# One more operand pair of a two-level Strassen-Winograd product goes by seven products instead of eight

## The chip, the cores and the metric

The kernel runs on one core of a Trainium2 chip. A core has five engines with a queue each: TensorE (PE, matrix products into PSUM), VectorE (DVE), ScalarE (ACT), GpSimd (POOL) and SyncE (SP). SP, ACT and POOL issue DMAs, which run on the core's sixteen DMA engines. PSUM has eight banks, and a 128x512 tile of float32 fills one. The metric is the device time of one launch in microseconds (us); less is better.

## The reference

A pre-norm block on x of 2 x 2048 x 512, in float32: x + attention(layernorm(x)), then x + feed-forward(layernorm(x)). The attention is over features, not positions, so it comes down to a few 512x512 products for each batch, and one product of all rows with a 512x512 matrix. The feed-forward is what the change touches:

```python
w = lut[idx]                      # 16 entries; gate, up: 1376 x 512, down: 512 x 1376
gate = einsum('bsh,oh->bso', x, w_gate)
up   = einsum('bsh,oh->bso', x, w_up)
h = silu(gate) * up
out = einsum('bsh,oh->bso', h, w_down)
```

## The kernel before

**Stages.** Layernorm and Gram matrices of x, the 512x512 products of the attention, its product with all rows (to about 287 us of the profile), gate and up (to 748 us), gate and up of the last 96 rows of the weights (to 790 us), the down product (to the end).

**Seven products for eight.** Two matrices cut in 2 x 2 blocks are multiplied by the Winograd form of Strassen's method: seven block products, named by their operand pairs 11·11, 12·21, 22·T4, S1·T1, S2·T2, S3·T3 and S4·22, and sums of blocks before and after. S are sums of blocks of the left operand (the weights), T of the right (the normed rows).

**Gate and up.** 11 tiles f of the weights' rows (the last one is short and goes another way), 4 pairs p of chunks of 1024 rows of x. The unit (f, p), class `GateUp`, makes gate and up of tile f for two chunks of 512 rows: the blocks' rows are gate and up, their columns the chunks, and the contraction (512) is cut in two. A block product is two matmuls of 128x128 weights with 128x512 rows. Stage methods `a1`, `c1`, `a2`, `c2`, `b`, `a3`, `a4` hold one block product each, with the copy out of PSUM (ScalarE) or the sum (VectorE) that follows; `silu`, `first`, `end`, `out` are the elementwise ends, which store h to DRAM from SP's queue.

**The second level.** From f = 2 on four units (f, p), (f, p+1), (f+1, p), (f+1, p+1), with f and p even, form a group, with the roles 0, 1, 2, 3. For one operand pair the products of the four units are again a 2 x 2 block product, of 128x128 and 128x512 blocks, so seven matmuls do for eight. Class `Second` does this for 12·21 (`of_b`), 22·T4 (`of_c`) and S4·22 (`of_d`). Its own right sums T1, T2, T4 are made once for each pair of p (`sums`, method `made`), put in DRAM (`far`) and loaded back for each group by ScalarE's queue (`load`). Its left sums are made for each pair of f (`sums_left`). A group runs role 0, role 1 (of both pairs of p), then roles 2 and 3. What roles 2 and 3 need of role 1's products (`r6`, `r5`) goes to DRAM: `part` copies the PSUM bank to SBUF and stores it from ScalarE's queue, role 2 adds to it with an accumulating DMA from GpSimd's queue (`onto=True`), and it comes back either with an accumulating DMA into a tile (`add_part`, of_b into `p1`, of_c into `u2`) or plain (`back`, of_d, into `y`), all from GpSimd's queue.

**Order.** The order on PE, ACT, DVE and SP is written out by hand: `Line.run` puts the stages of a unit among those of the unit before it. Between stages stands `between`, which issues one waiting load (`to_load`), one waiting set of sums (`todo`), and fills VectorE with the lookup of the weights (`fill`), as long as a planner's clock says that VectorE is less than `leads[0]` us ahead of TensorE. GpSimd's order is the framework's. DMAs of SP and ACT share eight semaphores in turn, those of POOL have eight others.

**Buffers.** PSUM: two banks "a", two "c", one each of "b", "x" (of_b), "z" (of_c), "w" (of_d). SBUF: eight buffers for T (`TT`), three for the copies of parts (`RT`), one each for `p1`, `p7`, `h1`, `y`. The class `LastRows` uses the rows again after of_b, of_c and of_d changed some blocks in place (`b12 = b22 - b12`), so it has weights of its own for the chunks concerned. The class `Down` runs through the same `Line`.

## Time and profile before

| what | value |
| --- | --- |
| median of 3 runs | 1063.71 us (1063.35 to 1063.77) |
| the profiled execution: its own time | 1064.37 us |
| its span, first to last instruction | 1062.6 us |
| instructions | 11343 |
| mean DMA rate over the span | 183 GB/s |
| a 128x512 sum on VectorE (L172), mean | 0.68 to 0.69 us |
| a 128x512 copy on ScalarE (L181, L1014), mean | 0.586 us |

The profile is of one execution. A group row has busy time, mean time of one, and the idle time of the engine before it with what ended it. An engine's idle time costs nothing unless the chain that ended last goes through it. Slices are 40 equal parts of the span; a digit is the busy share in tenths, PEclk the granted clock. A row of windows gives the length, then busy us of each engine with the number of its instructions, the granted clock, the mean busy share of the sixteen DMA engines and GB/s. A DMA issue is listed with the size and the median time from issue to landing.

### The profile page before, as it was taken

What the parts mean: (1) busy time and instruction counts of PE and PEld (TensorE: products, weight loads), DVE (VectorE), ACT (ScalarE), POOL (GpSimd) and SP (SyncE); (2) the same over time, 40 slices, a digit from 0 to 9 for tenths busy, and PEclk for the clock granted to TensorE, in tenths of its full rate; (3) what the DMA queues carried; (4) which work ended last, traced back from release to release, by engine and by line L of the source; (5) the groups of instructions that cost most, each with busy time, mean ns of one, the idle gap of its engine ahead of it and who ended that gap; (6) DMA issues with size and microseconds to landing.
All of it is one profiled execution on the core that took longest, in us unless ns stands there. A gap on an engine that the chain in (4) does not pass through costs nothing.

```text
span 1062.6 us, 11343 instructions
## 1 busy us (share of the span) xinstructions
PE 1055.5 (99%) x3554; PEld 661.3 (62%) x3554; DVE 803.3 (76%) x1538; ACT 385.1 (36%) x725; POOL 108.6 (10%) x160
## 2 busy tenths in 40 slices
PE   8999999999999999999999999999999999999998
PEld 5668887444444444444444444444998888888887
DVE  7888788898998897887988868849756455656554
ACT  4652532455542224444443444444222222211111
POOL 0000000012120120230141023014000000000000
PEclk9999999999999999999999999999999999999999
DMA  8650314589571366696697679569747665666773
GB/s 342 224 186 21 74 25 119 137 225 250 153 217 41 133 232 197 166 201 209 198 188 215 199 170 222 190 205 195 238 149 244 204 211 187 194 195 203 226 227 117
DMA packets 129084, 194.69 MB, mean 183 GB/s; under 512 B 18992, under 2 KB 59184, under 8 KB 127872
## 3 DMA queue, kind: packets, MB, share of 16 engines
q1 hardware_dynamic: 75904, 105.81, 31.4%
q0 software_dynamic: 15776, 39.92, 17.9%
q10 hardware_dynamic: 37344, 48.24, 14.0%
q8 instruction: 28, 0.46, 0.2%
q14 instruction: 32, 0.26, 0.1%
HBM read 111.42 MB, written 82.51 MB: 183 GB/s over the span
## 4 chain that ended last, share of the span: by engine, by line
PE 97%; DVE 1%; ACT 1%; DMA 0%; issue 0%; SPq 0%; ACTq 0%
PE a_g L1065 22%; PE a_d L1065 14%; PE y L839 10%; PE c_g L1065 8%; PE c_d L1065 7%; PE gp L522 6%; PE rows L1349 4%; PE b_d L1065 4%; PE x_g L1065 4%; PE z_g L1065 4%; PE w_g L1065 3%; PE b_g L1065 2%; PE ea_t L675 1%; PE ea_p L675 1%; PE ea_m L675 1%; PE ea_s L675 1%
## 5 line engine op out<-in xcount | busy, mean ns | idle before, releaser
L839 PE MATMUL y<-m,nT 128*128 128x512 f32 x256 | 110.2, 592 | 0.0
L342 DVE COPY_PREDICATED w<-b_w,w 128x1024 f32<-128x1024 int16 (+1 forms) x77 | 98.6, 1280 | 1.4
L839 PEld LDWEIGHTS y<-m,nT 128*128 128x128 f32 x256 | 48.5, 190 | 60.5 <-issue 57.3
L1065 PE MATMUL a_g<-xT_a,s 128*128 128x512 f32 x160 | 75.5, 594 | 0.0
L1065 PE MATMUL a_g<-xb,w 128*128 128x512 f32 x160 | 75.3, 593 | 0.0
L1065 PE MATMUL c_g<-xb,w 128*128 128x512 f32 x160 | 75.2, 592 | 0.0
L1065 PE MATMUL a_d<-dT,hs_a 128*128 128x256 f32 x288 | 72.6, 379 | 0.0
L522 PE MATMUL gp<-xn_a 128*128 128x128 f32 (+3 forms) x256 | 69.9, 434 | 1.7 <-DVE xn_a L223 1.7
L330 DVE TENSOR_SCALAR w<-idx_w,lut_x,lut_sb 128x1024 int32<-128x1024 int32 (+1 forms) x88 | 67.7, 794 | 0.2
L522 PEld LDWEIGHTS gp<-xn_a 128*128 128x128 f32 x256 | 43.9, 190 | 28.4 <-issue 15.1
L172 DVE TENSOR_TENSOR r<-r,p_d 128x256 f32<-128x256 f32 x64 | 27.1, 424 | 44.4 <-ACT p_d L181 41.5
L1065 PEld LDWEIGHTS a_d<-dT,hs_a 128*128 128x128 f32 x288 | 54.5, 189 | 7.7
L1065 PE MATMUL a_g<-xT_sq,s 128*128 128x512 f32 x120 | 56.7, 595 | 0.0
L181 ACT COPY p_d<-a_d 128x256 f32<-128x256 f32 x32 | 11.9, 372 | 121.4 <-PE a_d L1065 121.4
L1065 PEld LDWEIGHTS a_g<-xT_a,s 128*128 128x128 f32 x160 | 30.1, 190 | 38.9 <-issue 36.4
L1065 PEld LDWEIGHTS a_g<-xb,w 128*128 128x128 f32 x160 | 30.3, 190 | 38.5 <-issue 35.9
L1065 PEld LDWEIGHTS c_g<-xb,w 128*128 128x128 f32 x160 | 30.4, 190 | 38.3 <-issue 37.3
L342 DVE COPY_PREDICATED wd<-b_wd,wd 128x1024 f32<-128x1024 int16 (+1 forms) x42 | 50.7, 1208 | 0.8
L172 DVE TENSOR_TENSOR r<-r,a_d 128x256 f32<-128x256 f32 x64 | 26.8, 419 | 29.5 <-PE a_d L1065 29.5
L181 ACT COPY u<-a_g 128x512 f32<-128x512 f32 x40 | 23.4, 586 | 59.9 <-PE a_g L1065 57.3
L172 DVE TENSOR_TENSOR c<-a_g,p 128x512 f32<-128x512 f32 x40 | 27.6, 691 | 20.4 <-PE a_g L1065 19.0
L1349 PEld LDWEIGHTS rows<-last,xb 128*128 128x128 f32 x256 | 41.7, 190 | 0.5 <-issue 0.5
(357 smaller groups left out, 2086.2 us busy)
## 6 DMA issues: line engine op xcount, KB each, us to landing
hd<-h SPq DMA_DIRECT2D x80, 256.0 KB, 3.3
h<-hd SPq DMA_DIRECT2D x40, 512.0 KB, 6.3
nl<-nd SPq DMA_DIRECT2D x32, 256.0 KB, 5.8
xnd<-xn_f ACTq DMA_DIRECT2D x16, 512.0 KB, 4.6
fl<-xnd POOLq DMA_DIRECT2D x32, 256.0 KB, 6.1
xn_back<-xnd SPq DMA_DIRECT2D x32, 256.0 KB, 4.0
rd<-r SPq DMA_DIRECT2D x32, 256.0 KB, 3.2
r<-rd SPq DMA_DIRECT2D x32, 256.0 KB, 4.5
```

The source lines that it names most:

```text
L172: nc.vector.tensor_tensor(dest, a, b, op)
L181: nc.scalar.copy(dest, a)
L330: vec.tensor_scalar(dest.bitcast(I32), idx, lut_x[:rows, k : k + 1], lut_i[:rows, at : at + 1], ALU.bitwise_and, ALU.bitwise_xor,)
L342: vec.copy_predicated(dest, masks[level - 1], t)
L522: nc.tensor.matmul(gp[b][i][:, i * P :], xn[:, i, j % 2, :], xn[:, i:, j % 2, :], start=c % CPB == 0 and j == 0, stop=c % CPB == CPB - 1 a ...
L675: nc.tensor.matmul(ps[:, m, :], self.a[a][:, k, m * P : (m + 1) * P], self.b[b][:, k, :], start=first and m == k == 0, stop=k == 1, skip_g ...
L839: nc.tensor.matmul(ys[k], nTs[k][:, i, :], m[:, i, :], start=(i == 0), stop=(i == KB - 1))
L1065: nc.tensor.matmul(ps, lhsT, rhs, start=first and i == 0, stop=i == len(pairs) - 1, skip_group_check=not first,)
L1349: nc.tensor.matmul(ps[:, jj, :], x[:, j * P : (j + 1) * P], w, start=i == 0, stop=i == len(pairs) - 1,)
```

## The change

S3·T3 becomes a fourth `Second`, `of_e`, with the PSUM bank "e", which "c" gives up. In role 0 its first product is copied from "e" to "c" (`c0`), and `c1` adds to it there; role 1 has two kept products of it and `e4`, roles 2 and 3 get their S3·T3 as returns of `of_e` into `p7` (asked for by SP's queue before the unit begins, two buffers), role 2 with `e3` added. `of_d`'s returns go into `h1` (two buffers, SP's queue) and `y` is gone. T has five buffers instead of eight, and the loads of a group come in two lots: five in the unit before role 1, the rest within it. The copies of parts have four buffers, which the making of T uses too. `Line.run` is written anew for the roles. The planner's lead is 1.7 instead of 1.4 us. `LastRows` gets one more sum, since of_e changes T3 in place, and its sums are put on the list after the first product of the last rows.

```diff
     def psum(tag, name):
-        return fps.tile([P, E], F32, tag=tag, name=name, bufs=2 if tag in "ac" else 1)
+        return fps.tile([P, E], F32, tag=tag, name=name, bufs=2 if tag == "a" else 1)
...
-                r[tag] = x2p.tile([P, CH], F32, tag="tt", name=f"{tag}_{self.name}{g}", bufs=TT)
+                r[tag] = x2p.tile([P, CH], F32, tag="rt", name=f"{tag}_{self.name}{g}", bufs=RT)
...
-        def back(self, u):
-
-            t = u.temp("y")
-            nc.gpsimd.dma_start(t, self.parts[u.p // 2, {2: "r6", 3: "r5"}[u.role]])
+        def back(self, u, tag):
+            t = u.temp(tag, 2)
+            nc.sync.dma_start(t, self.parts[u.p // 2, {2: "r6", 3: "r5"}[u.role]])
             return t
-    RT, TT = 3, 8
+    RT, TT = 4, 5
...
-    seconds = [of_c, of_b, of_d]
+    of_e = Second("e", "e", lambda f: in_two(gu[f]["S3"]), lambda p: in_two(xs[p]["T3"]))
+    seconds = [of_c, of_b, of_e, of_d]
...
+    def loads(f, p, late=False):
         g = p // 2
+        order = []
         if 1 < f < NFT - 1 and f % 2 == 0 and p % 2:
-            order = [(of_c, "T2"), (of_c, "T1")]
-            order += [(o, tag) for tag in ("T2", "T1") for o in (of_d, of_b)]
-        elif 1 < f < NFT - 1 and f % 2 and p % 2 == 0:
-            order = [(o, "T4") for o in seconds]
+            order = [(o, tag) for tag in ("T2", "T1") for o in (of_c, of_e)]
+            order += [(of_d, "T2"), (of_b, "T2"), (of_d, "T1"), (of_b, "T1")]
+            order = order[TT:] if late else order[:TT]
+        elif 1 < f < NFT - 1 and f % 2 and p % 2 == 0 and not late:
+            order = [(o, "T4") for o in (of_e, of_b, of_c, of_d)]
...
         def c1(self):
-            self.c = self.view("c")
-            mm(self.c, self.pairs("S3", "T3"), True)
-            self.p7 = self.temp("p7")
+            if self.role is None:
+                self.c = self.view("c")
+                mm(self.c, self.pairs("S3", "T3"), True)
+            else:
+                mm(self.c, of_e.pair(self, "12", "21"), False)
+            self.p7 = self.temp("p7", 2)
             evict(self.p7, self.c)
...
+        def c0(self):
+            of_e.begin(self, "11", "11")
+            self.c = self.view("c")
+            evict(self.c, of_e.ps)
+        def kept(self, o, a, b, tag, onto=False):
+            (o.begin if onto else o.go_on)(self, a, b)
+            o.part(self, tag, onto)
+        def c4(self):
+            of_c.go_on(self, "S4", "22")
+            add(self.u2, of_c.ps, self.u2)
+        def e4(self):
+            of_e.go_on(self, "S4", "22")
+            self.p7 = self.temp("p7", 2)
+            evict(self.p7, of_e.ps)
+            add(self.u2, of_e.ps, self.u2)
+        def e3(self):
+            of_e.go_on(self, "22", "T4")
+            add(self.p7, of_e.ps, self.p7)
+        def c3(self):
+            of_c.go_on(self, "22", "T4")
+        def y_kept(self):
+            add(self.h1, of_d.ps, self.h1)
...
         def run(self, u, final=False):
...
+            after = before == 3 and role == 0
+            if not after:
+                of_last("silu")
             u.a1()
+            if role == 3:
+                u.h1 = of_d.back(u, "h1")
+                last.c3()
+                last.y_kept()
+                go(0.0)
+                u.a2()
+                go(0.0)
+                of_last("a4", "first")
+                go(0.0)
+                last.end()
+                go()
+                last.out()
+                u.a3()
+                go()
+                u.b()
+                go()
+                return
+            go()
             if before == 1:
                 last.first()
+            if role == 1:
+                u.kept(of_c, "S2", "T2", "r6")
+                go()
+                u.kept(of_e, "S2", "T2", "r6")
+            elif role == 2:
+                u.kept(of_c, "S3", "T3", "r5", True)
+                go()
+                u.kept(of_e, "S3", "T3", "r5", True)
+                u.kept(of_b, "S3", "T3", "r5", True)
+            else:
+                u.c1() if role is None else u.c0()
+                if after:
+                    last.silu()
+                go()
+            if last is not None:
+                last.a4()
+                if role == 2:
+                    u.h1 = of_d.back(u, "h1")
+                go()
+            if role == 1:
+                u.kept(of_c, "S1", "T1", "r5")
+            u.a2()
+            go()
+            if before == 3:
+                last.first()
+            if role == 1:
+                u.kept(of_e, "S1", "T1", "r5")
+                u.kept(of_d, "S2", "T2", "r6")
+                u.kept(of_b, "S2", "T2", "r6")
+                u.c4()
+            elif role == 2:
+                u.kept(of_d, "S3", "T3", "r5", True)
+                u.e3()
...
+            if role == 1:
+                u.e4()
+                u.kept(of_d, "S1", "T1", "r5")
+                u.kept(of_b, "S1", "T1", "r5")
...
-    leads = [1.4]
+    leads = [1.7]
...
-        to_load[:] = loads(*following)
+        to_load[:] = loads(f, p, late=True) + loads(*following)
...
-        u = GateUp(f, p)
+        u = next_unit or GateUp(f, p)
         line.run(u)
+        next_unit = GateUp(*following) if following[0] < NFT - 1 else None
+        if next_unit and next_unit.role in (2, 3):
+            next_unit.p7 = of_e.back(next_unit, "p7")
```

## The prediction

> **What bounds the kernel now.** I read the page first (busy shares, slices, the chain that ended last), then the chain in order of time, then the windows by stage, the DMA queues of one stretch, and the timeline of ScalarE where a unit hands over to the next.
>
> ```profile
> PE 1055.5 (99%) x3554; PEld 661.3 (62%) x3554; DVE 803.3 (76%) x1538; ACT 385.1 (36%) x725; POOL 108.6 (10%) x160
> ...
> PEclk9999999999999999999999999999999999999999
> DMA  8650314589571366696697679569747665666773
> ...
> PE 97%; DVE 1%; ACT 1%; DMA 0%; issue 0%; SPq 0%; ACTq 0%
> ```
>
> TensorE is busy 99% of the span at full granted clock, and the chain is TensorE for 97% of it. No other engine is over 76%. One piece of the chain gives the price of a product:
>
> ```profile
> 180.06 106.44 PE y L839 x248
> ```
>
> Each product has two records, so 128x512 costs 106.44 / 124 = 0.858 us. The gate-and-up units run back to back (a window row: span, then busy us of PE, PEld, DVE, ACT, POOL, then clock, DMA share, GB/s):
>
> ```profile
> 290.00:380.00 90.00, 90.00 (x211) 39.66 (x210) 81.28 (x118) 29.45 (x50) 13.34 (x24) 1.00 0.44 137
> 400.00:748.00 348.00, 348.00 (x812) 153.21 (x811) 283.54 (x424) 151.30 (x256) 71.58 (x89) 1.00 0.75 197
> ```
>
> From 400 to 748 us, where units go in groups of four, TensorE has no gap at all. A product taken out there is worth its 0.858 us, unless something that was covered comes out.
>
> **Removed: eight products.** A group has 56 products less one for each operand pair that already goes by seven (12·21, 22·T4, S4·22): 53. With S3·T3 it is 52. There are four pairs of f and two of p, so eight groups: the instruction lists have 699 products of 128x512 before and 691 after. 8 x 0.858 = 6.87 us, all on the path, and no more, since TensorE has no gap in this stage that could close besides. Group by role (0 to 3): 14, 17, 14, 8 products before, 14, 18, 14, 6 after. So roles 2 and 3 shrink from 22 to 20 products, 18.9 to 17.2 us, and role 1 grows.
>
> The Trainium skill, page Perfetto Trace Analysis, section Identifying the Most-Contended Engine, says that matmul busy time is a poor measure and weight loads are a good one. They fill 153.21 of 348 us here, so by the page TensorE has room and the sum could be 0; the row of 348.00 busy in 348.00 and the even 0.858 us speak for 6.87.
>
> **Added on VectorE and ScalarE.** VectorE gets 16 more 128x512 (0.69 us), 16 of 128x128 (0.28) and one of 128x192 (0.35): 15.9 us. Eight of the large ones and the first four of the small are a one-time set of sums near 380 to 410; the others are 2.5 us in each 91 us of a pair of f. VectorE is idle 64 of 348 us, so cover is there; without it 15.9 us is the most. ScalarE gets 16 more copies at 0.586 (9.4 us) and 40 more DMA issues at 0.33, on 151 of 348 us. The tightest place is role 1: eight kept copies, each followed by its store, in 18 products (15.4 us). Before, six followed each other as close as the matmuls came. Counting copies of 0.59 and issues of 0.45 from the rows, the last kept copy ends within 0.3 us of the product that needs its bank, when p is 3 and the cast of 1.03 us falls in there. I charge 0 and keep 0.3 x 4 = 1.2 us as its upper end. The lead of 1.7 for 1.4 lets VectorE queue 0.3 us more ahead of a result. The shortest way back is `c22` before the unit's own `a4`: in f 0 and 1 that sum ended at 298.5 and the `a4` began at 300.45, 1.9 us of cover; from f 2 on it is five products now, 4.3 us, where it was six or seven and f 0 has four. I charge 0.
>
> Bank "c" has one buffer now. In units of f 0 and 1 the sum that frees it started at 390.45 and took 0.69; the next `c1` began at 395.73. That is 4.6 us of cover; it costs nothing.
>
> **Right operands through five buffers.** Of eight T1 and T2 loads three go out within role 1. T2 of b waits on ScalarE's queue for the first z product (three products into the unit); behind it stands the copy of that very product, so nothing else is held up. It is used eight products later, 6.9 us. Landings of these loads had medians from 2.7 to 6.0 us: covered, by 0.5 us at worst.
>
> **Moved and added DMAs.** d's returns (16) go from GpSimd's queue to SP's, 16 returns of e join them there, GpSimd gets 8 accumulates more, ScalarE's queue 24 loads and 16 stores. A return waits on SP for the accumulate that feeds it; behind it stand the stores of h and the next return. In roles 2 and 3 this counts:
>
> ```profile
> 442.00:480.00 38.00, 38.00 (x89) 16.55 (x88) 33.46 (x57) 15.84 (x27) 13.55 (x17) 1.00 0.96 209
> ...
> 427.00:447.00 20.00, 20.00 (x48) 8.93 (x47) 17.62 (x22) 8.53 (x15) 5.61 (x7) 1.00 0.61 148
> ```
>
> ```profile
> q0 software_dynamic: 2272, 4.72, 72.0%
> q1 hardware_dynamic: 1080, 1.95, 14.4%
> q10 hardware_dynamic: 688, 1.27, 9.1%
> ...
> u<-part_r_c POOLq DMA_DIRECT2D x4, 256.0 KB, 5.1
> p<-part_r_b POOLq DMA_DIRECT2D x3, 256.0 KB, 4.7
> ...
> part_r_d<-r_d POOLq DMA_DIRECT2D x2, 256.0 KB, 7.2
> ```
>
> These are the DMA queues from 442 to 480 us, two times roles 2 and 3. The DMA engines are busy 0.96 of it. A plain 256 KB took (5.5 + 3.5) us / 3.22 MB, 0.73 us of all sixteen engines; GpSimd's queue had 27.4 us for 18 transfers by its bytes, 5 plain and 13 accumulating, so an accumulate is 1.8 us. The change adds here two accumulates (3.6), four returns (2.9) and a load (0.7) to 36.4 us: 43.6 us in a stretch that shrinks to 40 products, 34.3 us. Of the windows of 2 us from 436 to 492 us one had 1.21 and no other was over 1.10. At 1.05 the work lasts 41.5 us: some 7 us spill into roles 0 and 1, whose share was 0.61. They have the room; the question is who waits meanwhile.
>
> Two rules bear on this. The row is the share of 0.96, which leaves no second road. The skill's page DMA: Bandwidth & Descriptors, section Issuing engines are not separate DMA queues, says the same and speaks against the change: transfers from all queues interleave on the same sixteen engines, and moving returns to SP saves issue time only. The skill's page Perfetto Trace Analysis, sections Identifying the Most-Contended Engine and Engine Utilization, would judge DMA by HBM traffic instead, against 358 GB/s; 209 GB/s rising to an estimated 290 is below that, by which nothing is late and the gain is whole.
>
> The first to be hit is the hand-over from role 3 to role 2:
>
> ```profile
> 540.29 0.59 ACT L181 COPY p<-a_g 128x512 f32<-128x512 f32 x1 [2.08 <-PE a_g L1065]
> ...
> 547.09 0.63 ACT L1183 ACTIVATE h<-p 128x512 f32<-128x512 f32 x1 [1.15 <-DMA p<-part_r_b]
> 548.16 0.59 ACT L181 COPY p<-a_g 128x512 f32<-128x512 f32 x1 [0.43 <-PE a_g L1065]
> ```
>
> ScalarE waits at the Silu for the accumulate into p1; behind it stands the next unit's copy of p1, and TensorE's `a2` waits for that. Role 3 began at 538.38, that `a2` at 551.34: 12.9 us. Now role 3 has 8 products and `a2` comes after 5 more: 11.2 us. The copy ends 2.5 us in; the accumulate landed 4.8 us after its issue (542.27 to 547.09), so at 7.3, or 0.9 later like another one (450.02 to 455.7); Silu, copy and 0.2 of handover end at 8.7 to 9.6. Slack: 1.6 to 2.5 us, where it was 2.8. By that place about half of the spill, 3.5 us, has built up, but much of it is stores of h and loads for the next unit. So a stall is between 0 and 2 us for each of the four pairs of f. I take 0.27, near the lower end, since before no wait in these stretches reached TensorE. Role 3 before role 0 has its Silu later, behind one more product, and `a2` needs no such copy behind it: 0. The returns: e's is asked for before the unit begins and read after `e3`, ten products in (8.6 us), against landings of 4.6 to 5.1 us of d's returns before; where VectorE still waits, `c22` stands behind it, and TensorE writes its bank again eight products after `e3`. d's for role 3 waits on SP for an accumulate of role 2 and may land 1 to 2 us late; what is late then is a bank that TensorE needs 13 products on. Both 0.
>
> **Sum.** Against the profiled execution's own 1064.37 us (span 1062.6, 1.77 outside): 1064.37 - 6.87 + 4 x 0.27 = 1058.6. That execution stood 0.66 over the median of 1063.71, so 1057.9.
>
> **Rivals.** *DMA late (slower).* The accumulate into p1 lands over 2 us later than before, ScalarE sits at the Silu, TensorE at `a2`. Price if the 7 us spill reaches TensorE but for 2 us of slack: 4 x 5 = 20 us, 1077. It decides from 1.7 us for each pair (6.87 / 4). For it: 43.6 us of transfers in 34.3. Against: half of them have no reader near, and the landings of 4.7 to 7.2 us before were at a share of 0.96 already. *Gain eaten (no change).* 1.2 to 2.2 us for each pair, from that stall, ScalarE's tight role 1 and late returns together; or products that go without TensorE getting shorter. 1061.6 to 1065.8. Against: 348.00 busy in 348.00.
>
> **How the numbers follow.** Measurement tells 0.2% (2.1 us) from no change. Forecast, 0.76: 1056.3 (whole gain, less the half us by which runs differ) to 1061.5. Gain eaten, 0.10. DMA late, 0.14. The range 1056.3 to 1063.5 leaves out the last and half of the second. Faster 0.76, same 0.10, slower 0.14.
>
> **What would show it.** Right: 104 products in each pair of f, 89.3 us where it was 91.2; TensorE busy in all of the stage; DMA share near 1.0 in roles 2 and 3 and above 0.7 in 0 and 1. Wrong: TensorE waits for ScalarE's p1 copy behind a Silu that waits for a DMA; then the landing of p1's accumulate is over 7 us.

## The result and the profile after

The changed kernel took 1069.05 us (median of 4, 1067.85 to 1070.81), the kernel before 1063.65 in the same comparison (1063.35 to 1063.77). The ratio is 1.0053, interval 1.0035 to 1.0070: slower by half a per cent. Forecast were 1057.9 us, 1056.3 to 1063.5, and "faster" with 0.76.

The profiled execution took 1067.85 us (span 1066.1), the fastest of the four: it is 3.5 us over the one of the kernel before where the medians are 5.4 apart, so some 2 us of the loss are not in this trace. First the page of the changed kernel: its busy shares and its DMA slices.

```profile
PE 1052.6 (99%) x3538; PEld 655.6 (62%) x3538; DVE 815.5 (76%) x1571; ACT 390.9 (37%) x741; POOL 107.2 (10%) x158
...
DMA  8750314589671376896798699679847665666773
```

The sixteen matmul records are gone (3554 to 3538) and TensorE is still called 99% busy, so this part of the page doesn't say where the time went. The starts of TensorE's records do: in gate and up they follow each other by 0.429 us where nothing holds them. From the first record of gate and up to the first of the last rows it was 461.22 us before and is 465.23 now, 4.01 more. Sixteen records less are 6.87; so 10.88 us of gaps came in. Summed up, all that exceeds 0.429 was 1.17 us before and is 12.05 now: 39 gaps of 0.06 to 0.15 us (10 before) with 3.7 us in all, and ten longer ones with 8.2. The stages behind kept their lengths (down: 269.38 and 269.38 us between its first record and its last); gate and up began 0.5 us sooner. TensorE's waits in the changed kernel (us in total, times, longest) name the longer ones:

```profile
PE a_g L1065 <- ACT p L181: 3.7, 2, 2.8
PE a_g L1065 <- DVE h L172: 1.9, 3, 1.1
...
PE c_g L1065 <- ACT p L181: 0.7, 1, 0.7
```

Windows: one pair of f of the changed kernel, its two times roles 2 and 3, and those of the kernel before. The columns are those of the windows in the prediction.

```profile
400.00:491.00 91.00, 90.28 (x207) 38.06 (x206) 74.56 (x122) 41.28 (x71) 17.29 (x21) 1.00 0.85 250
436.00:472.00 36.00, 35.97 (x84) 15.30 (x83) 28.98 (x43) 14.64 (x26) 14.06 (x17) 1.00 1.01 257
```

```profile
436.00:472.00 36.00, 36.00 (x85) 15.69 (x83) 31.22 (x54) 16.05 (x27) 14.47 (x17) 1.00 0.90 187
```

The DMA share from 436 to 472 us is 1.01, where 0.90 was (the 0.96 of the prediction is from 442 to 480), and landings there are longer. The last column of these DMA issues, from 433 to 476 us of the changed kernel, is the median time from issue to landing:

```profile
hd<-h SPq DMA_DIRECT2D x7, 256.0 KB, 6.7
...
p<-part_r_b POOLq DMA_DIRECT2D x4, 256.0 KB, 5.5
h<-part_r_d SPq DMA_DIRECT2D x4, 256.0 KB, 6.4
u<-part_r_c POOLq DMA_DIRECT2D x4, 256.0 KB, 7.9
```

Before, from 436 to 480 us, the store of h took 3.9, p1's accumulate 4.5, d's return 5.1 and u2's accumulate 5.1. Now three kinds of place where a late landing or a short cover reaches TensorE. *A, a return of d.* The timeline of SP's queue, VectorE and TensorE at the end of the first pair of f:

```profile
464.66 0.32 SPq L1030 DMA_DIRECT2D h<-part_r_d  x1
```

```profile
470.93 0.69 DVE L172 TENSOR_TENSOR h<-w_g,h 128x512 f32<-128x512 f32 x1 [2.65 <-DMA h<-part_r_d]
471.54 0.28 DVE L172 TENSOR_TENSOR lc<-w 128x128 f32<-128x128 f32 x1
...
473.20 0.28 DVE L172 TENSOR_TENSOR lb<-w,lb 128x128 f32<-128x128 f32 x1
473.40 0.68 DVE L172 TENSOR_TENSOR h<-a_g,h 128x512 f32<-128x512 f32 x1
```

```profile
474.13 1.98 PE L1065 MATMUL a_g<-xb,w 128*128 128x512 f32 x4 [0.48 <-DVE h L172]
```

The return loads into h1, which has two buffers. It is issued at 464.66, when the store of h from two units before has landed, and lands 6.3 us later. VectorE waits for it in `y_kept`. Behind that stand eight small sums of the fillers and then the sum of `a4`, which frees bank "a" for the next f's `a1`. The same pattern costs 0.65 us here, 1.28 at 565 and 0.49 at 656.

*B, p1's accumulate.* Timelines of GpSimd, ScalarE and TensorE at the last hand-over from role 3 to role 2:

```profile
728.35 0.87 POOL L1026 DMA_DIRECT2D p<-part_r_b  x1 [7.22 <-DMA part_r_b<-r_b]
```

```profile
735.55 0.63 ACT L1178 ACTIVATE h<-p 128x512 f32<-128x512 f32 x1 [5.97 <-DMA T_d_in<-far_d1T]
736.21 0.58 ACT L181 COPY p<-a_g 128x512 f32<-128x512 f32 x1
...
736.85 1.13 PE L1065 MATMUL a_g<-xT_a,s 128*128 128x512 f32 x2 [2.79 <-ACT p L181]
```

GpSimd issues the accumulate late, because it waits for b's own accumulate in DRAM; it lands after 7.2 us, ScalarE has waited 5.97 us at the Silu, and p1's copy behind it holds TensorE. (The profile names the load that ended at the same time; the Silu reads only p1.)

*C, one product of cover.* TensorE through a role 3, first before, then after:

```profile
466.19 1.88 PE L1065 MATMUL a_g<-xb,w 128*128 128x512 f32 x4
467.91 1.88 PE L1065 MATMUL c_g<-xb,w 128*128 128x512 f32 x4
469.63 1.88 PE L1065 MATMUL a_g<-xT_x,s 128*128 128x512 f32 x4
```

```profile
466.45 1.88 PE L1065 MATMUL a_g<-xb,w 128*128 128x512 f32 x4
468.17 1.02 PE L1065 MATMUL z_g<-T_c_in,w 128*128 128x512 f32 x2
469.03 1.96 PE L1065 MATMUL a_g<-xT_x,s 128*128 128x512 f32 x4
```

Between `a1` and `a2` ScalarE copies the bank (0.58). Before, `c1` stood between with two products, 1.72 us; now it is `c3` with one, 0.86. Copy and hand-over fill that to the edge: `a2` takes 1.96 for 1.88, one of the 39 small gaps, and whatever else ScalarE has in hand goes straight to TensorE: 1.05 us at 746, where two copies of the last rows' weights stand before p1's copy. The kernel before shows the same mark: eight of its ten small gaps are at `a3` of role 3, where only one product stands between `a2` and `a3` in both kernels.

Bank "c" in role 0 is another such place. Its copy into `p7` stands between `c1` and `c2`. TensorE in the third unit of f = 8 (role 0 of its second group), before and after, then ScalarE after:

```profile
684.74 1.02 PE L1065 MATMUL c_g<-xb,w 128*128 128x512 f32 x2
...
688.17 1.02 PE L1065 MATMUL z_g<-xT_sq,w 128*128 128x512 f32 x2
689.03 1.02 PE L1065 MATMUL c_g<-xT_sq,w 128*128 128x512 f32 x2
```

```profile
688.09 1.02 PE L1065 MATMUL c_g<-xb,w 128*128 128x512 f32 x2
688.94 1.02 PE L1065 MATMUL z_g<-xT_sq,w 128*128 128x512 f32 x2
690.70 1.13 PE L1065 MATMUL c_g<-xT_sq,w 128*128 128x512 f32 x2 [0.74 <-ACT p L181]
```

```profile
689.12 1.04 ACT L303 CAST b_wd<-idx_wd 128x1024 int16<-128x1024 int32 x1 [0.25 <-DMA idx_wd<-in_down_idx_dram]
690.07 0.58 ACT L181 COPY p<-c_g 128x512 f32<-128x512 f32 x1
```

Before, `a4` and `a2` stood between as well; now only the product into "z" does. In seven of the eight roles 0 `c2` has a small gap of 0.085, and here, where a cast stands before the copy, it is 0.9 late.

### The profile page after: what moved, and what is told of

Read it like the earlier page. It is cut to its first block, busy times and chain, and to the rows that moved or that the text cites. A ratio compares the mean times of both kernels' runs of the same rounds, so it can differ in the third digit from the quotient of the medians.

```text
span 1066.1 us, 11473 instructions
## 1 busy us (share of the span) xinstructions
PE 1052.6 (99%) x3538; PEld 655.6 (62%) x3538; DVE 815.5 (76%) x1571; ACT 390.9 (37%) x741; POOL 107.2 (10%) x158
## 5 line engine op out<-in xcount | busy, mean ns | idle before, releaser
L1065 PEld LDWEIGHTS a_g<-xb,w 128*128 128x128 f32 x160 | 30.1, 190 | 41.4 <-issue 34.9
L172 DVE TENSOR_TENSOR h<-a_g,h 128x512 f32<-128x512 f32 x32 | 22.1, 689 | 35.7 <-ACT h L181 19.6
L1383 PE MATMUL rows<-last,xb 128*128 128x192 f32 x256 | 41.8, 326 | 0.0
L1065 PEld LDWEIGHTS a_g<-xT_sq,s 128*128 128x128 f32 x120 | 22.2, 190 | 29.8 <-issue 25.1
```

The lines of the kernel that those rows point to most:

```text
L172: nc.vector.tensor_tensor(dest, a, b, op)
L1065: nc.tensor.matmul(ps, lhsT, rhs, start=first and i == 0, stop=i == len(pairs) - 1, skip_group_check=not first,)
L1383: nc.tensor.matmul(ps[:, jj, :], x[:, j * P : (j + 1) * P], w, start=i == 0, stop=i == len(pairs) - 1,)
```

## The experiments

Each run was timed over some rounds beside the kernel before. "Over before" is the median less the median of before in the same comparison; the changed kernel stands at +5.4. Excess is the sum of the gaps in gate and up in the profiled execution (1.17 before, 12.05 in the changed kernel). The theory I began with: the DMA engines are overfull in roles 2 and 3, and the late landings are the stalls. The rival: the order and the covers on ScalarE and VectorE.

| run | median us | ratio, 95% interval | over before | excess |
| --- | --- | --- | --- | --- |
| e_no_traffic | 1066.72 | 1.0025 [1.0016, 1.0035] | +2.9 | 11.4 |
| e_no_accum | 1068.68 | 1.0041 [1.0030, 1.0053] | +4.9 | 14.8 |
| e_loose_return | 1069.55 | 1.0051 [1.0038, 1.0063] | +5.7 | 12.8 |
| b_first | 1070.21 | 1.0062 [1.0050, 1.0074] | +6.4 | 13.8 |
| no_sums_by_dma | 1062.82 | 0.9989 [0.9981, 0.9998] | -1.0 | 6.3 |
| y_late | 1066.88 | 1.0028 [1.0019, 1.0038] | +3.1 | 14.0 |
| h1_three | 1068.77 | 1.0043 [1.0030, 1.0056] | +4.9 | 13.3 |
| p1_two_silu | 1080.34 | 1.0149 [1.0131, 1.0168] | +16.5 | 25.9 |
| before_busy | 1065.14 | 1.0011 [1.0002, 1.0020] | +1.3 | 2.4 |
| banks | 1079.23 | 1.0148 [1.0133, 1.0163] | +15.4 | 13.7 |
| tuned | 1066.05 | 1.0031 [1.0020, 1.0042] | +2.3 | 9.6 |
| best | 1078.43 | 1.0135 [1.0119, 1.0152] | +14.6 | 15.6 |
| d_ahead | 1070.80 | 1.0059 [1.0047, 1.0071] | +6.9 | 15.5 |
| t_late | 1067.92 | 1.0037 [1.0025, 1.0049] | +4.0 | 12.1 |
| pad | 1073.16 | 1.0084 [1.0071, 1.0097] | +9.3 | 11.1 |
| tuned2 | 1066.28 | 1.0031 [1.0018, 1.0045] | +2.4 | 10.6 |
| tuned3 | 1063.81 | 1.0007 [0.9999, 1.0016] | +0.05 | 7.7 |
| tuned4 | 1062.90 | 0.9994 [0.9986, 1.0003] | -0.9 | 6.9 |

The profiled execution can lie up to 3 us off its median (y_late's took 1069.8), so medians decide, and the excess shows where. The runs e_no_traffic, e_no_accum, e_loose_return and no_sums_by_dma leave out transfers or sums that the result needs; they are there to find the stalls and are no versions of the kernel.

### Is it part e's transfers?

**e_no_traffic**

```diff
             nc.scalar.copy(t, self.ps)
+            if self is of_e:
+                return
...
-            add(self.p7, of_e.ps, self.p7)
+            add(self.p7, of_e.ps, self.old)
...
-            next_unit.p7 = of_e.back(next_unit, "p7")
+            next_unit.old = u.p7
+            next_unit.p7 = u.p7 if next_unit.role == 3 else next_unit.temp("p7", 2)
```

> Left out: the two stores, the accumulate and the two returns that part e makes in each group (the copies on ScalarE and all products stay; role 2 sums over an old p7 instead, role 3 reads role 2's). That is 4.7 us of DMA time for each group by the prices of the prediction, some 6.5 us of it in the two roles 2 and 3 of one pair of f. Theory 'load' (the sixteen DMA engines have more work in roles 2 and 3 than time, so landings that TensorE waits for through ScalarE and VectorE are 2 to 3 us later): DMA share in roles 2 and 3 falls from 1.01 to about 0.85, landings fall back under 6 us, the 10.9 us of stalls mostly go, 1057.5 to 1061. Rival 'order' (ScalarE and VectorE get more work and in a worse order, whatever the DMAs do): the copies and sums are all still there, so 1067 to 1070.

It fell between: 2.5 us of 5.4 came back, and 11.4 us of excess stayed. The share from 436 to 472 us went only to 0.97 (231 GB/s) and d's returns still took 6.5 us; e's loads of right operands stayed in. I had expected 0.85: what is left, 37.1 us of transfers by the prices of the prediction (43.6 less 6.5), still stands in roles that were cut to 34.3 us.

**e_no_accum** left out the one accumulate, **e_loose_return** replaced e's returns by copies that nobody waits for, **b_first** changed two products in order.

```diff
-            if onto:
+            if onto and self is of_e:
+                return
```

> Left out: only the accumulate of part e's S3 T3 product onto the kept part (one 256 KB transfer in each group, priced at 1.8 us of all sixteen engines); its copy, the stores and the returns stay. Theory 'load': 3.6 us less in a stretch of 36 us with a share of 1.01, so about 0.92, a little under the 0.96 of the kernel before, and p1's accumulate lands sooner; half to most of the stalls go, 1060 to 1065. Rival 'order': no change, 1067 to 1070. A third view, that it is GpSimd's queue where p1's accumulate stands behind this one: as with load, but the DMA share then stays near 1.0.

```diff
-            add(self.p7, of_e.ps, self.p7)
+            add(self.p7, of_e.ps, self.old)
...
-            next_unit.p7 = of_e.back(next_unit, "p7")
+            next_unit.old = u.p7
+            next_unit.p7 = u.p7 if next_unit.role == 3 else next_unit.temp("p7", 2)
+            spare = dram.tile([P, CH], F32, tag=f"spare_{next_unit.name}", name=f"spare_{next_unit.name}")
+            nc.sync.dma_start(spare, of_e.far[next_unit.p // 2, "T1"])
```

> Part e's returns are replaced by copies of 256 KB from and to DRAM on the same queue at the same place, which wait for nothing and for which nobody waits (role 2 sums over an old p7 instead, role 3 reads role 2's p7); stores and accumulate stay. The DMA load stays or grows a little, e's own waits on SP's queue and at VectorE are gone. Theory 'load': 1066 to 1070. Rival 'the returns themselves' (they hold up SP's queue, and with it stores of h and d's returns, or VectorE waits for them): 1059 to 1064.

```diff
-                u.kept(of_e, "S3", "T3", "r5", True)
                 u.kept(of_b, "S3", "T3", "r5", True)
+                u.kept(of_e, "S3", "T3", "r5", True)
```

> Only the order of two products in role 2 with their copies and accumulates: b's S3 T3 before e's, so that b's accumulate, which feeds p1's in role 3, is issued one product and one transfer sooner. Nothing is taken out. Theory 'load' with the predicted hand-over as its main outlet: p1's accumulate lands 1 to 2.5 us sooner in role 3, the waits of TensorE for ScalarE's p1 copy (about 4 us in all) go, d's returns (about 3 us) and ScalarE's other delays stay: 1063.5 to 1066. If the wait for p1 is only one of many outlets and the engines stay as full: within 1 us of the changed kernel, 1068 to 1070.

All three stayed at the changed kernel's time, within their intervals. So neither e's accumulate nor the waits for its returns nor its place ahead of b is the cause alone; e's stores and loads were not tried by themselves.

**before_busy**, the kernel before with transfers in place of e's stores, returns and accumulate (the returns by stores of the same size; e's loads are not added):

```diff
         u = GateUp(f, p)
+        for i in range({1: 2, 2: 1, 3: 1}.get(u.role, 0)):
+            t = dram.tile([P, CH], F32, tag=f"spare_{u.name}_{i}", name=f"spare_{u.name}_{i}")
+            nc.sync.dma_start(t, xs[p]["11"][:, 0, :])
+            if u.role == 1 and i == 0:
+                spare = t
+        if u.role == 2:
+            nc.gpsimd.dma_start(spare, xs[p]["11"][:, 1, :], accum_op=ALU.add)
         line.run(u)
```

> The kernel before with the transfers of part e added and nobody waiting for them: in each group two plain 256 KB stores at the start of role 1, one at the start of role 2, one at the start of role 3 (SP's queue) and one accumulate (GpSimd's queue) in role 2, all to spare places in DRAM. In roles 2 and 3 that is about 6.5 us on top of 36.4 us, in a stretch that stays 38 us long. Theory 'load alone': the engines are as overfull as in the changed kernel but for the 4 us of length, so stalls as there, 1066 to 1070. Rival 'load times short covers': in the kernel before two products and not one stand between the steps of role 3, y is a buffer of its own and the fillers do not stand behind the wait, so late landings are mostly covered: 1063.5 to 1065.

It lost 1.3 us, and its only longer gap is one of 1.2 us. But it is a weaker test than I meant. Its window and its DMA issues (436 to 480 us):

```profile
436.00:472.00 36.00, 36.00 (x85) 15.72 (x84) 30.76 (x55) 16.17 (x27) 14.33 (x17) 1.00 0.97 221
```

```profile
p<-part_r_b POOLq DMA_DIRECT2D x4, 256.0 KB, 5.2
...
spare<-xb SPq DMA_DIRECT2D x3, 256.0 KB, 6.2
```

The share is 0.97 (0.90 without them), and the store of h landed in 3.9 us as before, p1's accumulate in 5.2 for 4.5: these transfers alone made the others hardly later. So this run shows that the added traffic costs little in roles of the old length, and not how the old order would stand late landings.

### Without any sum by DMA

**no_sums_by_dma**

```diff
-                nc.gpsimd.dma_start(self.parts[g, tag], t, accum_op=ALU.add)
...
-                nc.gpsimd.dma_start(dest, self.parts[u.p // 2, tag], accum_op=ALU.add)
...
-            t = u.temp(tag, 2)
-            nc.sync.dma_start(t, self.parts[u.p // 2, {2: "r6", 3: "r5"}[u.role]])
-            return t
+            return u.temp(tag, 2)
...
```

> Left out: every accumulate and every return of a kept part, of all four parts b, c, d and e (sums that took them read an old tile instead); all products, copies, stores of kept parts and loads of right operands stay, and so does the order on every engine. After the run without e's transfers (1066.7, share still 0.97 in roles 2 and 3) the load alone explains 2.3 of some 12 us. Theory 'transfers' (TensorE's stalls all come through a wait for an accumulate or a return, which land late because the shortened roles 2 and 3 are full): with none left the share falls below 0.7 and all stalls go but for a few tenths, 1057 to 1059.5. Rival 'short covers' (in the shortened role 3 one product, 0.86 us, stands between a step and the next on the same bank, with a ScalarE copy of 0.59 in between, and any other instruction on ScalarE or VectorE goes straight to TensorE): half or more of the stalls stay, 1061.5 to 1065.

The window of roles 2 and 3, and TensorE's waits in gate and up:

```profile
436.00:472.00 36.00, 36.00 (x84) 15.46 (x83) 30.59 (x50) 14.62 (x25) 1.06 (x2) 1.00 0.37 121
```

```profile
PE c_g L1061 <- ACT p L181: 0.9, 1, 0.9
PE a_g L1061 <- ACT p L181: 0.9, 1, 0.9
```

This run splits the loss. With the share at 0.37 and nobody waiting for a part, A and B are gone, 6.2 us under the changed kernel. But 6.3 us of excess remain, where the kernel before has 1.2: 33 small gaps (3.3 us), 0.4 us at one product of role 1, and two single ones that have nothing to do with a part. At 687 us a cast of 1.04 us on ScalarE, which waited 0.46 for its own load, stands before the copy that `c2` needs. At 740 us the two copies of the last rows' weights (0.5 each) stand before p1's copy in the last role 3. Before, the same two copies ended 1.04 us ahead of that copy's turn. So the rival holds for some 5 us, and what comes with the transfers for the other 6.

### The places, one at a time

**y_late** (A, by order) and **h1_three** (A, by a buffer):

```diff
-                last.y_kept()
                 go(0.0)
                 u.a2()
                 go(0.0)
+                last.y_kept()
```

> Only VectorE's order in role 3: the sum of d's product with its return, which waits for the return's landing, is put behind the fillers and directly before the sum that frees bank a, where it stood ahead of the fillers (12 sums of 0.28 us). Nothing is taken out, no transfer is moved. Theory: this wait with the fillers queued behind it is what delays a1 of the next f (0.74, 1.38 and 0.58 us with the refill, at 474, 565 and 656 us); these three stalls go, 1066 to 1067.5. Rival: the landing itself is what is late, and the bank waits for it in any order; then no change, 1068 to 1070.

```diff
-            t = u.temp(tag, 2)
+            if tag == "h1" and u.p == 2:
+                t = x2p.tile([P, CH], F32, tag="h1", name=f"h1_{u.name}")
+            else:
+                t = u.temp(tag, 2)
...
-    RT, TT = 4, 5
+    RT, TT = 4, 4
```

> d's return for the third unit of an odd f gets a buffer of its own (a third one, paid for with four buffers of right operands for five), so that its issue on SP's queue no longer waits for the store of h from two units before. Theory: the change brought this coupling in by loading the return into h1 instead of y; the return is issued some 6 us sooner, at role 2's start, and the three stalls at a1 of the next f (2.7 us) go, 1066 to 1068 as far as four buffers for right operands cost nothing. Rival 'load': the return lands late whenever it is issued, 1068 to 1070.5.

Both took away all three stalls of A. In y_late the return lands as late as ever, VectorE waits 0.89 us for it, and `a1` is on time, since the fillers (eight, not twelve) are ahead of the wait. The median is 2.3 us lower; the intervals still touch at their ends, so the trace is the firmer evidence. In h1_three the return is issued at 458.99 instead of 464.66 and nobody waits for it; that the run stayed at +4.9 all the same goes with waits for loads of T_b (0.5 us) and with a stall B of 3.2 us that slowed TensorE's clock (last section). The buffer was paid for with one of T, and that price was not measured alone.

**p1_two_silu** (B, by a buffer and order), **d_ahead** (B, by cover), **t_late** (B, by load), **pad** (C, by cover):

```diff
-                self.p1 = self.temp("p1")
+                one = self.role == 3 and self.p == 1
+                self.p1 = x2p.tile([P, CH], F32, tag="p1", name=f"p1_{self.name}") if one else self.temp("p1")
...
-            after = before == 3 and role == 0
+            after = before == 3
...
                 u.kept(of_b, "S3", "T3", "r5", True)
+                if after:
+                    last.silu()
...
-    RT, TT = 4, 5
+    RT, TT = 4, 4
```

> p1 of the second unit of an odd f gets a buffer of its own (also paid for with four buffers of right operands for five), and its Silu is put on ScalarE behind the next unit's p1 copy and its three kept copies, so that a late accumulate into p1 holds up none of them. Theory: the predicted hand-over (Silu waits for p1's accumulate, the p1 copy behind it, a2 waits) holds the stalls at 460, 551, 642 and 737 us, some 0.3 to 3 us each and 4 us in all; they go, 1064 to 1066.5. Rival: the wait moves on to the next ScalarE copy (u2's) or to the VectorE sums that need the Silu, and TensorE stalls there, 1067.5 to 1070.

It missed both expectations: +16.5. The hand-over to role 2 was free, and the next one broke. VectorE, then ScalarE, in the third unit of f = 3:

```profile
468.65 0.69 DVE L172 TENSOR_TENSOR p<-e_g,p 128x512 f32<-128x512 f32 x1 [3.03 <-DMA p<-part_r_e]
...
469.86 0.69 DVE L172 TENSOR_TENSOR h<-x_g,p 128x512 f32<-128x512 f32 x1
```

```profile
470.57 0.63 ACT L1174 ACTIVATE h<-h 128x512 f32<-128x512 f32 x1 [6.33 <-DVE h L172]
471.11 0.57 ACT L181 COPY p<-a_g 128x512 f32<-128x512 f32 x1
```

e's return was issued at 457.70 and landed some 11 us later. Behind VectorE's wait for it stands b's sum, behind that on ScalarE a Silu, behind that p1's copy, and `a2` waits 3.4 us. Three waits of this kind each slowed TensorE's clock as well (last section), 5.4 us of the 25.9.

```diff
             if role == 1:
                 u.kept(of_c, "S1", "T1", "r5")
+            elif role == 2:
+                u.kept(of_d, "S3", "T3", "r5", True)
             u.a2()
...
             elif role == 2:
-                u.kept(of_d, "S3", "T3", "r5", True)
                 u.e3()
```

> Only an order in role 2: d's S3 T3 product with its kept copy and accumulate goes ahead of a2, so that four products and not three stand between a1 and a2, where p1's copy has to be made. Theory 'short covers': each of the four stalls at the hand-over shrinks by up to one product, 0.86 us, 2 to 3 us in all, and d's returns come 1.7 us sooner: 1065.5 to 1067. Rival 'load': the landing of p1's accumulate slips further by what d's earlier accumulate takes, 1068 to 1070.

The stalls at the hand-over to role 2 of the second group were gone in the three later pairs of f, yet the run gained nothing (its interval overlaps that of the changed kernel). At the first group d's product now waits for bank "w", which a copy of the unit before still reads, and starts 0.84 us late each time, and in the profiled execution `a2` of the last role 3 came 3.65 us late:

```profile
PE w_g L1065 <- ACT h L181: 2.7, 4, 0.7
```

```diff
-        elif 1 < f < NFT - 1 and f % 2 and p % 2 == 0 and not late:
-            order = [(o, "T4") for o in (of_e, of_b, of_c, of_d)]
+        elif 1 < f < NFT - 1 and f % 2 and p % 2 == 0:
+            order = [(o, "T4") for o in ((of_c, of_d) if late else (of_e, of_b))]
```

> Only the loads of c's and d's T4, which are read in role 3, are asked for in role 2 and not in the unit before it: two plain loads of 256 KB (1.5 us of all sixteen engines) less beside p1's accumulate at the hand-over from role 3 to role 2. Theory 'load': p1's accumulate lands 1 to 1.5 us sooner than its 6 to 7.3 us, the four stalls at the hand-over shrink by 2 to 3 us in all, 1066 to 1067.5. Rival: the accumulates have their own queue and the loads only fill gaps, so no change, 1068.5 to 1070; or c's T4 lands late in role 3, then 1070 and more.

1.4 us better, but its interval and that of the changed kernel overlap: inconclusive. Two hand-overs to role 2 were free of stalls, the later two were not.

```diff
                 last.c3()
+                mm(u.view("c"), u.pairs("11", "11")[:1], True)
```

> One product that nobody reads is added to each role 3 between c3 and a2, into PSUM bank c, which is free there: eight products, 6.87 us of TensorE, back to the number of the kernel before. Theory 'short covers': it stands where p1's copy is made, so most of it fills stalls and the 0.085 us bubbles at a2, and gives the transfers in roles 2 and 3 as much more time; the time rises by 0 to 3 us only, 1069 to 1072. If the stalls have nothing to do with the length of role 3: 1075 to 1077.

+3.9 us for 6.87 us of product, between the two expectations. In the first pair of f the wait at `a2` is bought off: its small gap at 451.9 and 469.5 is gone (`a2` takes 1.88 again). By the medians some 3 us of the product filled gaps. The trace shows it less cleanly: the stalls A are gone and those of B are down to 0.3 us, but some 6 us of gaps stand at places that were free or nearly so (320, 405, 602, 684 and 719 us), and the excess fell by 0.9 only.

### Versions

**tuned**, **tuned2**, **tuned3** and **tuned4** change nothing but the order. All four have y_late's edit and the first two below (`c1` ahead of the fillers, e's sum before c22) and put the last rows' copies elsewhere; from tuned2 on there are t_late's and d_ahead's edits (d_ahead's in tuned3 and tuned4 only where the unit before is of role 3), from tuned3 on the last two below (the Silu behind p1's copy), and in tuned4 `b` directly behind `e3`:

```diff
             u.a2()
+            if role == 0:
+                u.c1()
...
-            add(self.p7, of_e.ps, self.p7)
...
             mm(self.a, self.pairs("S1", "T1"), False)
+            if self.role == 2:
+                add(self.p7, of_e.ps, self.p7)
...
-            after = before == 3 and role == 0
+            after = before == 3 and role == 0 or role == 3
...
             if role == 3:
+                last.silu()
```

> Four changes of order to the changed kernel, no transfer and no sum more or less: d's sum with its return behind the fillers (1066.9 alone), e's sum with its return directly before the sum c22, the two ScalarE copies of the last rows' weights behind the last unit, and c1 of role 0 ahead of the fillers, so that a cast on ScalarE doesn't stand before its copy. Theory 'short covers': the two single stalls that stayed with all sums by DMA left out (some 1.1 us each at the last unit and at the first role 0 of f = 8) go too, 1064 to 1066. Rival: what is taken from one place comes back at the next hand-over, since the transfers stay late, 1066.5 to 1068.

> All changes of order together, no transfer and no sum more or less than in the changed kernel: those of the run tuned (1066.05; the copies of the last rows' weights now behind u2's copy of the last unit and not behind the unit, where they cost 1.1 us), d's product ahead of a2, and c's and d's T4 asked for in role 2. If covers and load at the hand-over both count: 1061 to 1063.5, at or under the kernel before. If the stalls only move on: 1064.5 to 1066.

> The run tuned2 (1066.28) with two changes of order: d's product goes ahead of a2 only where the unit before is of role 3, so that the wait for bank w at the first hand-over of each pair of f (four times 0.84 us) goes, and the Silu of role 2 stands on ScalarE behind the p1 copy of role 3 and not ahead of it. If the stalls are a matter of these covers: 1061 to 1063.5. If late landings find the next short cover: 1064 to 1066.5.

> As tuned3, and in role 2 the b product with its sum into h0 goes directly behind e3, ahead of the fillers and of the last unit's h, so that p1 is read, and free for role 3's copy, about a us sooner. Covers: 1060.5 to 1063. If b's sum now waits for p1's accumulate with the last unit's sums queued behind it: 1064 to 1067.

tuned came out at the edge of both expectations: the wait for the cast went (`c2` is on time at 690 us), but the last rows' copies, put behind the unit, now made the first product of the last rows wait 1.1 us. tuned2 mended that and took over d_ahead's four waits for bank "w". tuned3, without them, is 5.3 us under the changed kernel and within 0.2% of the kernel before; so is tuned4, with one of its eleven runs at 1059.74. Its window and its landings (433 to 476 us) beside those of the changed kernel:

```profile
436.00:472.00 36.00, 35.40 (x83) 15.01 (x82) 30.91 (x50) 14.25 (x25) 14.28 (x17) 1.00 1.01 247
```

```profile
p<-part_r_b POOLq DMA_DIRECT2D x4, 256.0 KB, 5.4
h<-part_r_d SPq DMA_DIRECT2D x4, 256.0 KB, 5.1
u<-part_r_c POOLq DMA_DIRECT2D x4, 256.0 KB, 7.5
```

The share is still 1.01, p1's accumulate still lands in 5.4 us and u2's in 7.5; only d's return is sooner (5.1 for 6.4). The same transfers, as many copies and sums, and about 6 us less: most of what was lost went through the order, that is, through what stands behind a wait and what is asked for when. What stays of the excess, 6.9 us, is 3.2 of small gaps and three stalls of B with 2.8, at the second group. In this execution the last rows took 1.8 us longer too (43.2 us from first to last record, 41.4 in the changed kernel), a wait for VectorE.

**banks** and **best** took three of the eight accumulates in each pair of f out of the DMAs and gave VectorE twelve sums more in all:

```diff
...
-                u.kept(of_e, "S3", "T3", "r5", True)
-                u.kept(of_b, "S3", "T3", "r5", True)
+                u.held(of_e, "S3", "T3", "c")
+                if u.p == 0:
+                    u.held(of_b, "S3", "T3", "b")
+                else:
+                    u.kept(of_b, "S3", "T3", "r5", True)
```

> Three of the eight accumulates onto kept parts in each pair of f are taken out with the result kept the same: e's S3 T3 product of role 2 is copied into PSUM bank c, and b's of the first group into bank b (both banks are free in roles 1 to 3), and role 3 adds them on VectorE (p7, and h0 before the Silu). 5.4 us less of DMA in a stretch of 34.3 us, and p1's accumulate in the second unit needs to wait for no other accumulate. Theory 'load and its chain': the waits of TensorE behind p1's accumulate (0.3 to 3 us at each of the four hand-overs) and d's late returns shrink, 1064 to 1066.5. Rival: the waits move on to the next transfer, or the three sums more on VectorE cost as much, 1068 to 1070.5.

> The three accumulates into PSUM banks instead, the four changes of order, and the Silu of the second unit behind the next unit's p1 copy and kept copies. If load and short covers are both needed for the stalls, both are eased: 1060 to 1063, under the kernel before for the first time; the sum of products alone allows about 1058.5 with the 0.085 us bubbles of role 3 (some 2.5 us) on top. If the waits only move on: 1064 to 1067.

Both missed both expectations, by 8.7 and 11.4 us at the least. TensorE's waits in banks:

```profile
PE c_d L1065 <- DVE h L172: 4.1, 2, 2.9
PE e_g L1065 <- DVE le L172: 3.3, 2, 1.8
```

The twelve sums are 8.3 us. The planner fills VectorE up to its lead, so my reading, not tried alone, is that what no longer fits is put off: e's left sums came late, and the down stage, where "c_d" waits for sums of h, went from 269.4 to 277.2 us.

## Why the prediction was wrong

**Removed, 6.87 us: right.** Sixteen records less at 0.429 us, and the stages around kept their lengths.

**What came instead of 1.08 us.** The forecast had 1.08 us of new gaps; the profiled execution has 10.88. By place: 3.4 at the hand-over from role 3 to role 2 (B), 2.7 behind d's returns (A), 3.7 at covers of one product (C), 1.1 in role 1, each with the small gap that follows it.

**DMA in roles 2 and 3: right in kind.** 43.6 us of transfers in 34.3 were forecast at a share of 1.05 with a spill into roles 0 and 1. The 36.4 us in it were measured from 442 to 480 us, some 6 us later than the roles; from 436 to 472 the share went from 0.90 to 1.01, and in roles 0 and 1 (three windows of 33 us) from 0.60 to 0.65 up to 0.66 to 0.68. The landing of p1's accumulate over 7 us, named as the sign of a wrong forecast, came at 728 us (7.2).

**Hand-over from role 3 to role 2, 4 x 0.27: mis-sized.** The mechanism came as described, but uneven: 0.2, under 0.1, about 0 and 2.95 us in the profiled execution, 3.2 in all for 1.08. The bounds of 0 to 2 for each were too narrow at the top, since I took a landing 0.9 us late and left out that GpSimd issues the accumulate only when b's own has landed.

**d's returns, charged 0: a step that failed.** I followed the return of role 3 to a bank that is needed 13 products on. The late one was role 2's: it now loads into h1, waits for a store of h, and the sum behind it frees a bank that is needed as soon as role 3's last three products are through. I named what is queued behind a waiting return on SP and not what is queued behind it on VectorE. 2.4 us in three stalls, which are gone in y_late.

**Covers that got shorter, charged 0 or not at all: the step that cost most.** I costed the removed products as time and looked for their cover in one hand-over only. In role 3, `c1` with two products had been cover for p1's copy before `a2`; one is left, and that cost 1.9 us (small gaps at seven of eight, 1.05 at the last rows' copies). "Bank c costs nothing" is the same mistake: I checked the sum that frees the bank (the row at 390 us, which is of f = 2 and not of f 0 and 1) and not the copy between `c1` and `c2` of role 0, which the new order left with one product of cover; 1.6 us (0.085 at seven, 0.9 at the cast). `a2` of role 0 has 0.2 more. no_sums_by_dma shows them all without the transfers (3.8 us). Charged with these 3.7 us alone, the forecast would have been 1061.6.

**ScalarE's role 1, 0 to 1.2 us: 1.1, by another cause.** It came in one place, at 404 to 410 us, where ScalarE's copies of the parts ran late; before the first of them ScalarE waited 0.81 us for a store of the one-time T sums, whose buffers the copies share. It is in no_sums_by_dma too (0.9).

**VectorE, five buffers, lead.** TensorE waited for no load of a right operand, and VectorE's 15.9 us found room. But the cover there was thinner than "64 us idle" sounded: 8.3 us more did not fit in banks. The lead was not tried alone.

**The rivals.** "Gain eaten" had the right description, a stall, ScalarE's order and late returns together, at 1061.6 to 1065.8; what came was 3.2 us over its end. "DMA late" had the right direction, but 1077 took the spill but for 2 us as a wait at one place of each pair of f. Neither is the cause by itself: without part e's stores, accumulates and returns half of the loss stays, without any sum by DMA half of the stalls stay, and with the order mended nearly all of the loss goes while the share is 1.01. That mending a cover in one place sent the wait on to the next (p1_two_silu, d_ahead) speaks for both acting together. Not settled is how the 6 us with the transfers divide between the share and the bunching of requests, since before_busy hardly made the landings later.

## What to carry to other kernels

A product that is taken out of a full engine is worth its full time only if nothing used it as cover: list, for every copy and sum between two steps on one bank, how many products stand between before and after, and what is ahead of it on its engine, the hand-overs away from the change included. Where an engine has to wait for a transfer, what stands behind the wait decides much of the loss; in y_late, putting the wait behind the fillers took three stalls away and moved no transfer. One product (0.86 us) over one copy (0.58 us) was not a free cover here: charge a small gap each time (0.07 to 0.1 us in these runs), and whatever else that engine may be asked to do there.

## What the runs showed of the hardware

A long wait can cost TensorE more than its length. In y_late TensorE's records stopped for 2.6 us at 643 (idle for 2.45 by the profile) and then came 0.85 us apart instead of 0.43; the window shows the granted clock:

```profile
642.00:652.00 10.00, 7.55 (x14) 2.98 (x13) 5.82 (x12) 5.11 (x9) 5.77 (x6) 0.83 1.07 260
```

```profile
645.65 3.17 PE L1065 MATMUL a_g<-xT_a,s 128*128 128x512 f32 x4 [2.45 <-ACT p L181]
```

Four records went by at that pace, 1.6 us on top. In gate and up it came after stops of 2.6, 2.9, 3.2, 3.4, 3.7, 4.2 and 6.1 us in five runs, and not after one of 2.95 or any of 2.3 and less. The Trainium skill, page TensorE: Matmul & The Clock Gate, section What's actually happening, tells of a gate that falls to half the clock after an idle window of about 3.4 us that runs on its own: the half and the uneven onset agree with these rows, the 2.6 us lie below its figure. The slowing may be one reason why these kernels scatter by 2 to 6 us from run to run where the kernel before mostly stays within 1; that was not tried.
